# A graph attention kernel: a chunk's last product finished behind the next chunk's first block, its maxima transposed a half-step later, masks and sums loaded earlier

## The chip, the cores and the metric

The kernel runs on one core of a Trainium2 chip. A core has a matrix engine (TensorE, PE in the profile; PEld is its weight load), a vector engine (VectorE, DVE), a scalar engine (ScalarE, ACT), a general engine (GpSimd, POOL) and a queue engine (SyncE, SP) that issues most of the DMAs here. The metric is the time of one execution on the device in microseconds; lower is better.

## What is computed

There are 2708 nodes with 512 features each, and an adjacency matrix `adj` with 0 and 1, about 16 neighbours a node. Four layers follow each other, each with a residual and a layer norm. Layers 0, 1 and 3 multiply by `adj` (scaled by degrees in the first two) and by one 512 x 512 weight. Layer 2 is two attention layers, and this is where the change lies:

```python
def _gat_layer(x, W, adj):
    proj = x @ W
    Wh, Ws = jnp.split(proj, 2, axis=-1)
    scores = Wh @ Ws.T
    a = jax.nn.softmax(scores, axis=-1) * adj
    out = a @ Wh
    out = out + x
    return jax.nn.leaky_relu(out, NEG_SLOPE)
```

The softmax runs over all 2708 nodes before the mask is applied, so all scores must be made, with their maxima and sums; of the products `a @ Wh` only those at neighbours are needed.

## The kernel before, in words

**Tiling.** The nodes are 22 blocks of 128 rows (the last has 20). Their columns are cut into six chunks: 0 to 3 of 512, chunk 4 of 384, chunk 5 of 276. The scores are held transposed: for one chunk of columns, `ch.s[j]` is block j of rows. For each attention layer, `layer` (line 2105) goes through the six chunks, and while the scores of one chunk are made, the chunk before it is finished ("old" in the code), and the gathers of older ones are multiplied.

**The scores.** Chunks 0 to 4 ("seven") use a scheme of seven half products instead of eight. `pair_steps` (line 1694) takes two row blocks at a time, s and r. For a pair t, product numbers stand in `PRODUCTS` (line 1670). Each product is two matrix multiplications over half of the columns. They add up in two PSUM banks: y takes 2 and 3 in one half and 2 and 5 with it (`ahead`, then `six`), and x takes 1, then 6, 7 and 4 in turn. Between two of them ScalarE copies x out, since each partial sum is needed: after 1 and 6 into s, after 7 into v, after 4 into r. VectorE then adds y to s (`first_block`) and v to r (`second_block`). A pair is walked in two half-steps. In the first, `ahead` makes products 2 and 5 of this pair, VectorE runs `first_block` of the pair before, `one` makes product 1, and `four` makes product 4 of the pair two before. In the second, `seven` makes product 7 of the pair before, `six` makes 3 and 6 of this one, and VectorE runs `second_block` of the pair before. Each half-step yields "mid" once and "end" once. There are ten pairs; block 18 ("ALONE") and the small block 21 stand outside. They are made in `scores` (line 1788), ALONE ahead of the pairs and 21 after the first half-step. `walk` (line 2087) puts this in order. After the last pair, products 4 of the pair before, 7 and 4 of the last pair follow directly, and then the next chunk begins.

PSUM has eight banks in two halves of four. y lies in the first half, x in the first half for two pairs in three, and transposes and gathered sums in the second. A new tile takes the bank that has been free longest, and its writer waits for the last reader.

**The half-steps as a clock.** `layer` counts "end" in n: 0 after block ALONE, 1 to 20 for the half-steps, 21 after the last products. At n, besides the scores, it issues for the old chunk:

- `load_mask` (line 1869): four row blocks of the mask, one SP DMA of 256 KB at 512 columns, six a chunk
- `greatest` (line 1818): VectorE's running maximum over the row blocks, `top`. Blocks that are complete wait one call before they are taken, unless `last` is set
- `shift_rows` (line 1839): TensorE transposes `top` (tr_top), VectorE reduces it (mx) and spreads it (wide). `shift_columns` (line 1860): TensorE transposes it back (tr_mx), ScalarE copies it to `shift`
- `soften` (line 1876): one of SOFT = 26 calls. Call v subtracts `shift` from block v (VectorE); ScalarE takes the exponential of block v - 2; VectorE adds block v - 4 to the running sum and multiplies it by its mask, and SP writes it to the table `pairs` in DRAM. At chunk 5, which isn't "seven", nothing changes in this: the distance is that of the old chunk
- `weigh` (line 1989): GpSimd gathers rows of `pairs` by lists of neighbours (`fetch`, g in the profile, at most ten ahead), TensorE multiplies them (acc), VectorE ends the rows (xr, r). The two tables `pairs` are used in turn, so chunk k's writes must wait until chunk k - 2 has been gathered. A planner's clock, advanced by the cost of what TensorE is given, says when a gather counts as landed

For the following chunk it issues `load_moving` (xs, its moving columns, four SP DMAs), `sum_moving` (t1, t2, t4, six VectorE subtractions) and, in `pair_steps`, `load_sums` (s1, s2, s4, sums of weights of a group, three SP DMAs of 256 KB).

**Order.** Every engine and every queue runs its instructions in the order in which the program issues them: `Ordered` (line 54) ties each to the one before it on its engine. So an instruction that waits holds back what was issued after it on the same engine; SP's order holds masks, sums, xs and the writes of `pairs`.

**The end of attention.** After chunk 5 the rest of its softmax, gathers and products runs while TensorE is given other work (`fill`): in the first layer the projections of the second, in the second layer the beginning of layer 3, whose features are split into high and low halves (`halve` (line 749): xh by ScalarE, xl by VectorE) and whose adjacency bytes are cast to m by ScalarE.

In the profile nearly all instructions carry line 71, that of a helper, so its groups are told by the names of tiles.

Of the kernel before, what the change touches and what calls it, by code (L numbers as in the profile page):

```python
# [22 lines left out]
NB = 22  # L23
NP = NB * P
DC = D // P
# [463 lines left out]
SOFT = NB + 2 * 2  # L489
# [919 lines left out]
class Attention:  # L1409
# [7 lines left out]
    def __init__(self, fast):  # L1417
        self.f, self.k, self.nc = fast, fast.k, fast.nc
        self.page, self.bank = fast.page, fast.bank
        tc = self.k.tc  # L1420
        self.scratch = self.k.ctx.enter_context(
            tc.tile_pool(name="pairs", bufs=1, space=DRAM)
        )

        self.pairs = [
            [
                self.scratch.tile([NP, 2 * PAIR + D], FP, tag=f"p{a}{b}", name=f"pairs{a}{b}")
                for b in range(2)  # L1430
            ]
            for a in range(2)
        ]
        self.mixed = self.scratch.tile([DC, P, D], FP, tag="mixed", name="mixed")
        self.quarter = [
            [
                self.scratch.tile(
                    [2, P, pairs_of(k)[0] * P], FP, tag=f"q{a}_{k}", name=f"quarter{a}_{k}"
                )
                for k in range(len(CH))  # L1440
            ]
            for a in range(2)
        ]
        self.sums = [
            [
                self.scratch.tile([3, P, 2, 2 * P], FP, tag=f"u{a}_{k}", name=f"sums{a}_{k}")
                for k in range(STREAMED)
            ]
            for a in range(2)
        ]  # L1450
        self.layers = [AttentionLayer(a, self.pairs[a]) for a in range(2)]
        self.clock, self.fetch_free, self.pending = 0.0, 0.0, []


    def blank(self):
# [238 lines left out]
    def pair_steps(self, ch):  # L1694
# [7 lines left out]
        following = ch.k + 1 in SEVEN  # L1702
# [42 lines left out]
        for n, p in enumerate(pairs):  # L1745
            self.replace(ch.ly, p[0])
            if ch.k == 0 and p[0] in groups and p[1] == 0:
                self.keep_sums(ch.ly, p[0])
            t = begin(n, p)
            ahead(t)  # L1750
            if old:
                first_block(old)
            yield "mid"
            one(t)
            if older:
                four(older)
            if ch.k and p[1] == 0 and p[0] + 1 in groups:
                self.load_sums(ch.ly, p[0] + 1)
            if following and p == pairs[-1]:
                self.load_sums(ch.ly, 0)  # L1760
            yield "end"
            if old:
                seven(old)
            yield "mid"
            six(t)
            if old:
                second_block(old)
            older, old = old, t
            yield "end"
        four(older)  # L1770
        seven(old)
        first_block(old)
        yield "mid"
        four(old)
        second_block(old)
        yield "end"

    def load_moving(self, ch):
# [97 lines left out]
    def soften(self, ch):  # L1876


        nc, v, cw = self.nc, ch.softened, ch.cw
        ch.softened += 1  # L1880
        if v < NB:
            if v == 0 and ch.k >= 2:

                assert not self.chunks[ch.k - 2].to_fetch
            n = rows_of(v)
            s = ch.s[v][:n, :cw]
            nc.vector.tensor_sub(s, s, ch.shift[:n, :cw])
        j = v - ch.apart
        if 0 <= j < NB:
            s = ch.s[j][: rows_of(j), :cw]  # L1890
            nc.scalar.activation(s, s, AF.Exp)
        j -= ch.apart
        if j < 0:
            return
        if j == NB - 1:
            ch.softened = SOFT
        if j % DC == 0 and j + DC < NB:
            self.load_mask(ch, j // DC + 1)
        n = rows_of(j)
        s = ch.s[j][:n, :cw]  # L1900
        if j == 0:
            ch.sum = self.page(f"sum{ch.name}")
            nc.vector.tensor_copy(ch.sum[:, :cw], s)
        else:
            nc.vector.tensor_add(ch.sum[:n, :cw], ch.sum[:n, :cw], s)
        nc.vector.tensor_mul(s, s, ch.masks.pop(j)[:n, :cw])
        to = ch.ly.pairs[ch.k % 2][j * P : j * P + n, :]
        if cw == BANK:
            nc.sync.dma_start(
                to[:, : 2 * PAIR].rearrange("j (r x) -> j r x", x=PAIR)[:, :, D:],  # L1910
                ch.s[j][:n, :].rearrange("j (r x) -> j r x", x=2 * P),
            )
            return
        for r in range(2):
            w = min(2 * P, cw - r * 2 * P)
            nc.sync.dma_start(
                to[:, r * PAIR + D : r * PAIR + D + w],
                ch.s[j][:n, r * 2 * P : r * 2 * P + w],
            )
# [151 lines left out]
    def run(self, next_layer):  # L2071
# [11 lines left out]
        for ly in self.layers:  # L2083
            fill = self.second(chunks[1][0]) if ly.number == 0 else next_layer
            self.layer(ly, chunks[ly.number], fill)

    def walk(self, ch):

        if not ch.seven:
            for j in [0, 1, 2, NB - 1, *range(3, NB - 1)]:  # L2090
                self.scores(ch, j)
                yield "end"
            return
        if not ch.part:
            self.sum_moving(ch)
        self.scores(ch, ALONE)
        yield "end"
        n = 0
        for what in self.pair_steps(ch):
            yield what  # L2100
            n += what == "end"
            if what == "end" and n == 1:
                self.scores(ch, NB - 1)

    def layer(self, ly, chunks, fill):
        f = self.f
        self.chunks, self.made = chunks, {}
        for k, ch in enumerate(chunks):
# [3 lines left out]
            n = -1  # L2112
            for what in self.walk(ch):
                if what == "mid":
                    if old and n >= 2 and old.softened < SOFT:
                        self.soften(old)
                    continue
                n += 1
                if old and n == 0:
                    self.load_mask(old, 0)  # L2120
                    self.greatest(old, last=True)
                if old and n == 3 and k >= 3:
                    while chunks[k - 3].to_weigh:
                        self.weigh(True)
                if old and n >= 3:
                    for _ in range(n % 3 == 0 if ch.seven else 1 + n % 2):
                        if old.softened < SOFT:
                            self.soften(old)
                f.beat()
                if n == 14 and k:  # L2130
                    f.packed(k - 1)
                if following and n == 17:
                    self.load_moving(following)
                if following and following.seven and n == 20:
                    self.sum_moving(following)
                if not following and n in ((5, 11, 19) if ly.number == 0 else (5, 11)):
                    next(fill)
# [7 lines left out]
                for _ in range(3):  # L2145
                    if not self.weigh():
                        break
                if old and n == 1:
                    self.shift_rows(old)
                if old and n == 2:  # L2150
                    self.shift_columns(old)
            assert not old or old.softened == SOFT
        last = chunks[-1]
        self.load_mask(last, 0)
        self.greatest(last, last=True)
        self.until(self.clock + 3, fill)
        self.shift_rows(last)
# [119 lines left out]
```

## Time and profile before

| | |
|---|---|
| median of 3 runs | 2378.08 us (2374.12 to 2386.72) |
| the profiled execution | 2319.82 us |
| its span (first to last instruction) | 2317.6 us |
| attention's scores, layer by layer | about 769 to 1240 us and 1454 to 1933 us |
| mean granted TensorE clock | 0.986 |
| DMA | 523.27 MB, mean 226 GB/s |

The page shows one profiled execution. "Busy" is the share of the span in which an engine had an instruction under way; the ends of matmuls are modelled. In lists of waits, "PE spx <- ACT v" reads: TensorE's matmul that writes spx waited for ScalarE's instruction that wrote v. In a timeline, a line is start, duration, engine, line, operation, output <- inputs, shapes and a count, and in square brackets the idle time of the engine ahead of it with what ended that. Names: sp is a score block made directly; spy and spx are y and x of a pair; tr_top and tr_mx are the transposes of the maxima; a is a mask; g a gather; s<-s,shift, sum<-sum,s and s<-s,a are the three VectorE parts of `soften`; s<-s,spy is `first_block`, s<-s,v is `second_block`.

The chunks of the two layers begin (block ALONE, or the first block of chunk 5) near these times: 769, 837, 906, 1008, 1102 and 1171 us in the first, 1454, 1522, 1591, 1697, 1796 and 1868 us in the second. The profile took a window apart by engine; the prediction uses it.

### The profile page before, as it was taken

How to read it: one execution, taken by the hardware profiler on the slowest of the kernel's cores; microseconds unless marked ns; L12 is line 12 of the kernel's file. 1: busy time of each engine (PE TensorE's matmuls, PEld its weight loads, DVE VectorE, ACT ScalarE, POOL GpSimd, SP SyncE). 2: the span in 40 equal slices, each digit the busy share in tenths (PEclk: the TensorE clock that was granted, in tenths of full speed). 3: DMA queues.
4: the chain of work that ended last, by engine and by line, in shares of the span. 5: the costliest groups of instructions: out<-in, count | busy, mean ns of one | idle time of the engine just before them, and what ended most of it. 6: DMA issues, size and time to landing. Idle time of an engine off the chain costs nothing.

```text
span 2317.6 us, 29497 instructions
## 1 busy us (share of the span) xinstructions
PE 2234.1 (96%) x9724; PEld 1509.8 (65%) x9724; DVE 1549.7 (67%) x3180; ACT 727.9 (31%) x1654; POOL 702.0 (30%) x827
## 2 busy tenths in 40 slices
PE   9999999999999998999999999998999997999997
PEld 6677777777644786676855444786665763476685
DVE  6666787786664769888974522579888985355523
ACT  7444452222111233333422201243333432251211
POOL 2333441111000001635556550001635464643000
PEclk9999999999999999999999999999999998999999
DMA  9965762222557615879999999426978899884311
GB/s 338 280 201 164 191 187 84 76 80 92 208 195 275 213 41 189 313 277 341 318 341 340 364 364 391 167 75 211 309 258 309 314 322 340 260 259 143 112 47 43
DMA packets 285139, 523.27 MB, mean 226 GB/s; under 512 B 42926, under 2 KB 134758, under 8 KB 284976
## 3 DMA queue, kind: packets, MB, share of 16 engines
q1 hardware_dynamic: 216320, 306.34, 38.4%
q0 software_dynamic: 68656, 214.96, 27.9%
q8 instruction: 78, 1.28, 0.2%
q14 instruction: 85, 0.70, 0.1%
HBM read 335.34 MB, written 185.83 MB: 225 GB/s over the span
## 4 chain that ended last, share of the span: by engine, by line
PE 65%; DVE 15%; DMA 13%; issue 3%; ACT 2%; SPq 1%; POOL 1%; DVEq 0%; ACTq 0%; POOLq 0%
PE acc L71 27%; PE spx L71 9%; PE mm L71 8%; PE spy L71 7%; DVE s L71 6%; PE wst L71 5%; PE z L71 5%; DMA g<-pairs,givers 4%; PE sp L71 3%; DVE sum L71 2%; DMA pairs<-s 2%; DVE top L71 1%; DMA pairs<-z_sb 1%; DMA mask<-some 1%; DMA at<-in_adj_t 1%
## 5 line engine op out<-in xcount | busy, mean ns | idle before, releaser
L71 POOL DMA_INDIRECT g<-pairs,givers x510 | 520.4, 1020 | 894.3 <-issue 324.2
L71 PE MATMUL acc<-m,xh 128*128 128x512 f32 (+4 forms) x1584 | 568.7, 380 | 12.3 <-ACT m L71 11.3
L71 PE MATMUL acc<-m,xl 128*128 128x512 f32 (+4 forms) x1584 | 551.7, 366 | 10.1 <-DVE xl L71 10.1
L71 PEld LDWEIGHTS acc<-m,xh 128*128 128x128 f32 (+1 forms) x1584 | 289.4, 189 | 75.8 <-issue 21.2
L71 PEld LDWEIGHTS acc<-m,xl 128*128 128x128 f32 (+1 forms) x1584 | 289.7, 189 | 55.2 <-DVE xl L71 11.0
L71 PE MATMUL acc<-g 128*32 128x512 f32 (+1 forms) x1020 | 287.6, 611 | 11.6 <-DMA g<-pairs,givers 10.6
L71 PE MATMUL mm<-w,ht 128*128 128x512 f32 (+1 forms) x528 | 223.2, 593 | 0.0
L71 ACT CAST m<-at 128x512 fp32r<-128x512 uint8 (+5 forms) x396 | 198.7, 566 | 41.7 <-DMA at<-mask 26.8
L71 DVE TENSOR_TENSOR s<-s,a 128x512 f32<-128x512 f32 (+3 forms) x264 | 166.1, 629 | 55.5 <-DMA a<-mask 46.8
L71 PE MATMUL spx<-xs,wst_sb 128*128 128x256 f32 (+1 forms) x800 | 197.8, 372 | 2.6 <-DVE s L71 2.0
L71 PEld LDWEIGHTS acc<-g 128*32 128x32 f32 (+1 forms) x1020 | 78.7, 135 | 153.4 <-issue 91.8
L71 ACT ACTIVATE s<-s 128x512 f32<-128x512 f32 (+3 forms) x264 | 151.6, 581 | 76.3 <-DVE s L71 76.0
L71 PEld LDWEIGHTS spx<-xs,wst_sb 128*128 128x128 f32 x800 | 146.7, 190 | 41.9 <-ACT s L71 11.8
L71 PEld LDWEIGHTS mm<-w,ht 128*128 128x128 f32 (+1 forms) x528 | 95.8, 186 | 116.5 <-issue 112.8
L71 ACT COPY s<-spx 128x256 f32<-128x256 f32 (+1 forms) x300 | 107.7, 360 | 182.9 <-PE spx L71 182.8
L71 DVE TENSOR_TENSOR s<-s,shift 128x512 f32<-128x512 f32 (+3 forms) x264 | 161.4, 621 | 0.2 <-ACT shift L71 0.2
L71 DVE TENSOR_TENSOR sum<-sum,s 128x512 f32<-128x512 f32 (+4 forms) x252 | 156.6, 622 | 3.6 <-ACT s L71 3.6
L71 DVE TENSOR_TENSOR top<-top,s 128x512 f32<-128x512 f32 (+4 forms) x240 | 149.8, 624 | 4.9
L71 PE MATMUL wst<-xt,mixed 128*128 128x512 f32 (+2 forms) x384 | 151.7, 546 | 0.9 <-DMA xt<-t 0.9
L71 PE MATMUL z<-w,xt 128*128 128x512 f32 (+1 forms) x352 | 150.9, 595 | 0.0
L71 PE MATMUL sp<-xs,wst_sb 128*128 128x276 f32 (+5 forms) x512 | 134.3, 477 | 1.8 <-DMA xs<-t 1.8
L71 POOL DMA_DIRECT2D x<-o x44 | 26.0, 597 | 324.6 <-DVE o L71 320.4
(190 smaller groups left out, 2763.9 us busy)
## 6 DMA issues: line engine op xcount, KB each, us to landing
pairs<-z_sb SPq DMA_DIRECT2D x84, 768.0 KB
pairs<-s SPq DMA_DIRECT2D x168, 256.0 KB
s<-sums SPq DMA_DIRECT2D x96, 256.0 KB
at<-in_adj_t SPq DMA_DIRECT2D x84, 256.0 KB
xres<-x POOLq DMA_DIRECT2D x44, 256.0 KB, 4.8
x<-o POOLq DMA_DIRECT2D x43, 256.0 KB, 3.5
pairs<-s SPq DMA_DIRECT2D x84, 128.0 KB
a<-mask SPq DMA_DIRECT2D x40, 256.0 KB
```

Source lines behind the costliest of these rows:

```text
L71: ins = call(*args, **kw)
```

## The change

- The last product 4 and the last `second_block` of a chunk are no longer issued at its end. They are kept in `self.left` and issued by `end_pair` in the next chunk's walk, right after its first block.
- The last maxima are taken at n = 1 instead of 0, `shift_rows` runs at n = 2 instead of 1, `shift_columns` at 3 instead of 2. Softening begins at the second half-step of the second pair ("mid" at n = 3 instead of 2) and has calls at even n from 4 instead of at n divisible by three from 3. When the new chunk is chunk 5 it begins at n = 4 instead of 3, with one or two calls as before.
- Masks: groups 0 and 1 are loaded at n = 0 and 1, and each later group two groups ahead instead of one. At the end of a layer groups 0 and 1 of the last chunk are loaded together.
- The sums of the first group of the next chunk are loaded at the pair before the last instead of at the last. The next chunk's moving columns are loaded at n = 15 instead of 17, their sums made at 18 instead of 20.
- The loop at n = 3 that issued all remaining products of chunk k - 3 is gone. In its place, ahead of the first write of an old chunk's block to `pairs`, products of the chunk two before it are issued until none of that chunk's gathers is left to issue.

```diff
--- before.py
+++ after.py
@@ -1450,6 +1450,7 @@
         ]
         self.layers = [AttentionLayer(a, self.pairs[a]) for a in range(2)]
         self.clock, self.fetch_free, self.pending = 0.0, 0.0, []
+        self.left = None
 
 
     def blank(self):
@@ -1756,7 +1757,7 @@
                 four(older)
             if ch.k and p[1] == 0 and p[0] + 1 in groups:
                 self.load_sums(ch.ly, p[0] + 1)
-            if following and p == pairs[-1]:
+            if following and p == pairs[-2]:
                 self.load_sums(ch.ly, 0)
             yield "end"
             if old:
@@ -1770,9 +1771,12 @@
         four(older)
         seven(old)
         first_block(old)
-        yield "mid"
-        four(old)
-        second_block(old)
+
+        def rest():
+            four(old)
+            second_block(old)
+
+        self.left = rest
         yield "end"
 
     def load_moving(self, ch):
@@ -1879,9 +1883,6 @@
         nc, v, cw = self.nc, ch.softened, ch.cw
         ch.softened += 1
         if v < NB:
-            if v == 0 and ch.k >= 2:
-
-                assert not self.chunks[ch.k - 2].to_fetch
             n = rows_of(v)
             s = ch.s[v][:n, :cw]
             nc.vector.tensor_sub(s, s, ch.shift[:n, :cw])
@@ -1894,8 +1895,11 @@
             return
         if j == NB - 1:
             ch.softened = SOFT
-        if j % DC == 0 and j + DC < NB:
-            self.load_mask(ch, j // DC + 1)
+        if j == 0 and ch.k >= 2:
+            while self.chunks[ch.k - 2].to_fetch:
+                self.weigh(True)
+        if j % DC == 0 and j + 2 * DC < NB:
+            self.load_mask(ch, j // DC + 2)
         n = rows_of(j)
         s = ch.s[j][:n, :cw]
         if j == 0:
@@ -2084,16 +2088,24 @@
             fill = self.second(chunks[1][0]) if ly.number == 0 else next_layer
             self.layer(ly, chunks[ly.number], fill)
 
+    def end_pair(self):
+        if self.left:
+            self.left()
+            self.left = None
+
     def walk(self, ch):
 
         if not ch.seven:
             for j in [0, 1, 2, NB - 1, *range(3, NB - 1)]:
                 self.scores(ch, j)
+                if j == 0:
+                    self.end_pair()
                 yield "end"
             return
         if not ch.part:
             self.sum_moving(ch)
         self.scores(ch, ALONE)
+        self.end_pair()
         yield "end"
         n = 0
         for what in self.pair_steps(ch):
@@ -2112,26 +2124,23 @@
             n = -1
             for what in self.walk(ch):
                 if what == "mid":
-                    if old and n >= 2 and old.softened < SOFT:
+                    if old and n >= 3 and old.softened < SOFT:
                         self.soften(old)
                     continue
                 n += 1
-                if old and n == 0:
-                    self.load_mask(old, 0)
-                    self.greatest(old, last=True)
-                if old and n == 3 and k >= 3:
-                    while chunks[k - 3].to_weigh:
-                        self.weigh(True)
-                if old and n >= 3:
-                    for _ in range(n % 3 == 0 if ch.seven else 1 + n % 2):
+                if old and n < 2:
+                    self.load_mask(old, n)
+                    self.greatest(old, last=n == 1)
+                if old and n >= 4:
+                    for _ in range(n % 2 == 0 if ch.seven else 1 + n % 2):
                         if old.softened < SOFT:
                             self.soften(old)
                 f.beat()
                 if n == 14 and k:
                     f.packed(k - 1)
-                if following and n == 17:
+                if following and n == 15:
                     self.load_moving(following)
-                if following and following.seven and n == 20:
+                if following and following.seven and n == 18:
                     self.sum_moving(following)
                 if not following and n in ((5, 11, 19) if ly.number == 0 else (5, 11)):
                     next(fill)
@@ -2145,13 +2154,14 @@
                 for _ in range(3):
                     if not self.weigh():
                         break
-                if old and n == 1:
+                if old and n == 2:
                     self.shift_rows(old)
-                if old and n == 2:
+                if old and n == 3:
                     self.shift_columns(old)
             assert not old or old.softened == SOFT
         last = chunks[-1]
         self.load_mask(last, 0)
+        self.load_mask(last, 1)
         self.greatest(last, last=True)
         self.until(self.clock + 3, fill)
         self.shift_rows(last)
```

## The prediction

> **What bounds the kernel now.** I read the page first. TensorE is busy 96% of the span, nothing else comes near, and the clock is full but for one slice.
>
> ```profile
> span 2317.6 us, 29497 instructions
> PE 2234.1 (96%) x9724; PEld 1509.8 (65%) x9724; DVE 1549.7 (67%) x3180; ACT 727.9 (31%) x1654; POOL 702.0 (30%) x827
> PE   9999999999999998999999999998999997999997
> PEclk9999999999999999999999999999999998999999
> ```
>
> So only TensorE's idle time (83.5 us in all) and its half-clock stretches can be won. Next I asked for TensorE's waits in 770 to 1960 us, the attention stage, which the change touches alone. Columns: total us, times, longest.
>
> ```profile
> PE tr_top L71 <- DVE top L71: 12.1, 4, 5.2
> PE spx L71 <- ACT v L71: 10.1, 10, 3.5
> PE acc L71 <- DVE xl L71: 9.9, 1, 9.9
> PE acc L71 <- ACT m L71: 6.4, 1, 6.4
> PE acc L71 <- DMA g<-pairs,givers: 6.1, 6, 2.6
> PE spy L71 <- DMA s<-sums: 3.1, 3, 1.7
> PE sp L71 <- DMA xs<-t: 1.8, 3, 0.9
> ```
>
> These sit almost all at the ten changes of chunk and at the end of attention. Then the windows by chunk, here chunks 1, 2 and 4 of the first layer and one stretch inside a change of chunk (columns after the window: us, then busy us and count of PE, PEld, DVE, ACT, POOL, then granted clock and DMA share):
>
> ```profile
> 837.10:906.00 68.90, 66.98 (x305) 55.25 (x304) 62.45 (x105) 32.07 (x75) 0.00 (x0) 1.00 0.32 100
> 906.00:1007.90 101.90, 94.22 (x410) 64.01 (x409) 84.58 (x144) 30.94 (x74) 48.63 (x48) 0.97 0.85 297
> 1101.80:1170.80 69.00, 68.12 (x386) 55.63 (x385) 65.52 (x119) 29.84 (x78) 40.01 (x37) 1.00 0.94 332
> 915.40:922.30 6.90, 3.98 (x15) 1.79 (x16) 4.81 (x10) 0.00 (x0) 2.99 (x3) 0.51 0.79 240
> ```
>
> VectorE is at 91% in chunk 1 and 95% in chunk 4: there it nearly binds too. The last line shows the clock halved around a pause. The timeline at the change from chunk 1 to 2, and at the end of the second layer, shows who is late:
>
> ```profile
> 904.62 0.37 ACT L71 COPY v<-spx 128x256 f32<-128x256 f32 x1 [0.96 <-PE spx L71]
> 905.05 1.13 PE L71 MATMUL spx<-t,wst_sb 128*128 128x256 f32 x4 [0.46 <-ACT v L71]
> ...
> 915.45 0.68 DVE L71 TENSOR_TENSOR s<-s,a 20x512 f32<-20x512 f32 x1
> 916.06 2.20 DVE L71 TENSOR_TENSOR top<-top,s 128x512 f32<-128x512 f32 x3
> 918.32 1.11 PE L71 MATMUL tr_top<-ident,top 128*128 128x128 f32 x4 [5.18 <-DVE top L71]
> ...
> 1927.92 0.32 SPq L71 DMA_DIRECT2D a<-mask  x1
> 1935.48 0.56 DVE L71 TENSOR_TENSOR s<-s,a 128x384 f32<-128x384 f32 x1 [9.75 <-DMA a<-mask]
> 1949.98 0.80 PE L71 MATMUL acc<-m,xl 128*128 128x512 f32 x1 [9.86 <-DVE xl L71]
> ```
>
> Product 4 of a chunk's last pair waits for ScalarE's copy of product 7 (0.46 us). Five instructions of TensorE later the transposes of the maxima wait 5.18 us, because VectorE is still multiplying the last softened block by its mask at 915.45. Late in attention a mask load issued at 1927.92 holds VectorE until 1935.48, and layer 3's low halves (xl) stand behind it.
>
> **What the Trainium skill says.** "TensorE: Matmul & The Clock Gate", Part 1, says the clock falls to half after about one idle window of 3.4 us. The trace agrees: 0.51 over 6.9 us around the 5.18 us pause, and shorter pauses of 3.45, 3.05 and 2.61 us each carry one. "VectorE: DVE Perf Modes", section on the TRN2 errata, gives 691 ns for an fp32 tensor_tensor of 512; the trace has 0.68 to 0.69, but starts lie only 0.60 to 0.72 apart. "PSUM — Partial Sum Buffer", section on engine and sequencer instructions, says ScalarE and VectorE queues are strict FIFO: the trace agrees at 1935 us, where eight xl wait behind one mask product. "DMA: Bandwidth & Descriptors", Anatomy of one DMA, says that a DMA's wait is held by the issuing sequencer. SP's own waits agree: 52.3 us for DVE s between 1800 and 1960, with mask loads queued behind.
>
> **The change, part by part.** A product (four records, 256 columns) starts every 0.864 us at 797 us; seven make a pair, 6.05 us, walked as two half-steps. The first block of the next chunk (sp, eight records) takes 3.44 us (837.10 to 840.54), or about 2.6 us at 384 columns.
>
> *Product 4 behind the next first block.* Nothing is added: the same four matmuls (0.86), ScalarE copy (0.37) and VectorE addition (0.42) move. Between seven and four now lie 3.44 us of work that needs no copy, so the 10 waits on v (10.1 us) are covered: eight of about 0.45, one of 3.45 (needs all 3.44), one of 3.05 (2.6 covers it but for 0.45). About 9.6 us. The two long ones also hold a half clock of 3.4 us each: windows there have clock 0.64 over 4.7 us with TensorE busy, so 1.7 us lost each, 3.3 together. Value 12.5; bounds 3.6 (the small ones alone, if ScalarE stays blocked behind VectorE) and 13.4.
>
> *Maxima a half-step on.* TensorE gets the small last block (about 0.95) and two products (1.73) ahead of tr_top. That covers the waits of 0.47 and 1.28: 1.75 us. The two of 5.18 us are VectorE's backlog, which doesn't shrink: in 849.0 to 916.1 it is busy 64.4 of 67.1 us. Softening starts perhaps 0.6 us later, since the last block's 3.5 us of VectorE work now comes ahead of the transposed maxima. Last mask product then: 916.06 + 0.6 less the last pair's first addition (0.60), second (0.34) and two maxima (1.3), which now come after it: 914.4. That first addition frees a PSUM bank that product 1 of the next chunk needs: 915.1. TensorE is there at about 910.9, so a wait of some 4.2 us stays, under another name (spx waits for DVE s) and with a half clock. After it come 0.86 + 0.95 + 1.73, the transposes 0.5, two products 1.73: the second pair's product 1 starts near 921 where before it started at 925.75, less some 2 us of half clock. Of these 2.5 us, 1.2 are counted under product 4 and sums. I take 2 each, both layers: 4, with the 1.75 makes 5.5; bounds 0 and 12.1 plus two half clocks (half of 3.98 busy, 2.0 each) = 16.
>
> *Sums one pair earlier.* Three SP loads go out 6 us sooner, ahead of pairs<-s. Two waits of 0.69 go: 1.4. The third, 1.67, is the second group's, which isn't moved. Pages: at most 78 of 87 are live, so three more for a pair and one more mask fit: nothing, or up to 3 us if SP waits for a page with pairs<-s behind it.
>
> *Moving columns at 15, sums of them at 18.* Four SP loads. Chunk 5's in layer 0 were issued at 1161.33 and its last part kept TensorE until 1174.64; two half-steps sooner clears the 1.77 us and a half clock (0.61 over 4.4 us, 1.4): 3. Loads and sums keep their distance of three, so VectorE waits no longer for them. The six subtractions (2.6 us) cost VectorE the same earlier.
>
> *No forced weighing at step 3.* It stalls in chunk 5 alone: 2.61 + 1.7 half clock, 1.22. Later by several steps, when the gathers have landed: I take 3.5 of 5.5; lower bound 0. The new wait: pairs<-s of the old chunk's first block waits on SP for the last gather of the chunk two back, with mask loads behind it; gathers end near 1191 us and the block comes near 1195, so nothing, at worst a few us.
>
> *Masks two groups ahead.* Same six loads a chunk. A load goes out four blocks earlier in SP's order, so the one of 1927.92 goes out right behind layer 3's loads, near 1922.6, and the next near 1932 in place of 1937.49. VectorE's last wait ends near 1938 instead of 1942.88, and xl comes some 4.5 us sooner; with half clock 5. Bounds 0 and 16.2 + 2. Elsewhere mask waits fall where TensorE has other work: nothing.
>
> *Softening at a denser rate.* 26 calls remain, but between step 3 and 20 instead of 2 and 21. A block costs VectorE 1.93 us (subtraction at 897.62, the next at 899.55), a pair's own additions and maxima 2.27. With 3 calls for 2.67 a pair it is 8.06 against 7.4, where TensorE needs 6.05. In walks that VectorE binds, TensorE stalls on its banks mid-walk and has no use for VectorE's leisure later. At most two half-steps, 6 us, in each of chunks 1 and 4; for chunk 1 that is in the sum above. For the others I take 4 in all; bounds 0 and 19.
>
> Sum: 12.5 + 5.5 + 1.4 + 3 + 3.5 + 5 - 4 = 26.9 us. The profiled execution takes 2319.82 us (its span and 2.2 around it), so it would take 2292.9. The median shown is 58.3 above it; I take off the same microseconds: 2378.1 - 27 = **2351**.
>
> **The rivals.** *The waits only change names (2370).* ScalarE's v stays behind a late VectorE, the backlog decides chunk 1 in full, the tail stays bound by DMA. Left: eight times 0.45, 1.4 and 3, so 8 us. For it: VectorE at 91 to 95%. Against: 3.44 us of cover is plain work.
> *All the waits go (2320).* 13.4 + 16 + 1.4 + 3.2 + 5.5 + 18 = 58. Against: VectorE had no idle time in chunk 1.
> *VectorE's denser softening binds (slower, 2392).* Place: chunks 1 to 4, at the additions that free PSUM banks. Loss 2 x 6.05 in chunk 1, 2 x 6.6 in chunk 4, with weighing, 2 x 3 in chunks 2 and 3 of layer 1: 31. Maxima, weighing and tail then gain nothing, so against it stand 12.5 + 1.4 + 3: 14 net loss. It decides once TensorE's waits on DVE s exceed some 17 us more than the 4.4 of now. Against: total VectorE work is unchanged, and PSUM lets it lag about a pair.
>
> **Chances.** Forecast 0.55 (own range 2338 to 2363), names only 0.22 (2362 to 2380), all go 0.11 (2315 to 2338), denser binds 0.12 (2380 to 2410). A measurement of this kernel tells 0.5%, about 12 us, from no change. Faster by more: forecast, all go and a fifth of names only, 0.70; slower by more: two thirds of the last, 0.08; the rest 0.22. Range 2328 to 2384: it cuts about half of all-go and most of the last.
>
> **What would show it.** Right: no waits of spx on ACT v at chunk ends; tr_top waits under 1 us, with waits of spx on DVE s near 4 us in their place after chunk 1; no sp wait on xs near 1170; the acc wait on xl near 5 us. Wrong: new waits of spy and spx on DVE s inside walks over 9 us a chunk, SP waiting on gathers with VectorE on masks, or chunks 1 and 4 longer than 68.9 and 69.0 us.

## The result, and the profile after

The kernel after takes 2344.77 us (median; 2340.95 to 2348.78), beside it the kernel before 2379.68 (2374.12 to 2386.72): a ratio of 0.985, 95% interval 0.982 to 0.989. That is 34.9 us less; the forecast was 27 less.

One thing has to be known before any two times are compared: the runs of a group share one chip, and the unchanged kernel before took 2379.7, 2397.7 and 2385.1 us in three groups but 2319.4 and 2318.0 in two, so each kernel is set only against the runs of before in its own group.

The page of before (span 2317.6) is of the second sort, the first page of after (span 2339.0) of the first: subtracted from each other they would say 21 us slower. So the page of after used here is another one, from a group where before takes 2318.0 us (median). There after takes **2292.46** (median), 25.5 us less. The ratio on record for this group is 0.9908 (0.9886 to 0.9930), or 16 to 26 us; the two medians alone divide to 0.9890, which lies inside that interval. The prediction had worked out 2292.9 for such an execution. The page (label e5 below), to be laid beside that of before:

```profile
span 2288.4 us, 29486 instructions
PE 2215.9 (97%) x9724; PEld 1505.2 (66%) x9724; DVE 1547.3 (68%) x3180; ACT 727.7 (32%) x1654; POOL 718.4 (31%) x827
PE   9999999999999998999999999998999997999997
PEclk9999999999999999999999999999999998999999
```

The span is 29.2 us shorter. TensorE's idle time falls by 11.0 us (83.5 to 72.5), its busy time by 18.2 (2234.1 to 2215.9) with the same 9724 matmuls. Of these 18.2, 8.0 are the gathered products (acc<-g, 287.6 to 279.6; the reason is found at e4). Another part is the clock. In this pair of profiles the mean granted clock rises from 0.986 to 0.993, so the full-speed time lost falls from 0.014 x 2317.6 = 32 us to 16. But that is these two executions more than the change: over all runs of the group the mean clock is 0.989 for before and 0.990 for after, an estimate of some 25 and 22 us lost, so the clock makes some 3 us of the difference there.

The Trainium skill, "TensorE: Matmul & The Clock Gate", Part 1, says that the clock falls to half after about one idle window of 3.4 us. The trace agrees for the pause of 3.46 us below (clock 0.72 over the 7 us around it). In before, shorter pauses, of 2.61 and 3.05 us, brought a half clock too (0.62 and 0.64 over the 4.5 and 4.7 us around them), so here 3.4 us are not the least that is needed.

TensorE's waits in the attention stage of after (766 to 1956 us; columns as before: total, times, longest):

```profile
PE spx L71 <- DVE s L71: 9.9, 6, 3.8
PE acc L71 <- DVE xl L71: 9.6, 1, 9.6
PE spy L71 <- DVE s L71: 8.6, 3, 3.5
PE acc L71 <- DMA g<-pairs,givers: 5.6, 10, 1.1
PE acc L71 <- ACT m L71: 5.2, 1, 5.2
PE spy L71 <- DMA s<-sums: 3.1, 3, 1.6
PE spx L71 <- ACT v L71: 2.4, 2, 1.8
```

The waits of tr_top on top (12.1) are gone, and those of spx on v fell from 10.1 us to 2.4. What is left of these stands one product earlier: 1.78 us at 1768.29, ahead of the last product 4 that is still made inside the walk. In their place stand 18.5 us of waits on DVE s, 4.4 before. The one for xl is as long as it was (9.6 and 9.9).

The windows by chunk: chunks 1, 2 and 4 of the first layer, and then 7 us in the middle of chunk 1 (columns as in the prediction):

```profile
831.17:905.00 73.83, 69.18 (x305) 57.18 (x304) 64.15 (x109) 31.99 (x75) 0.00 (x0) 0.95 0.37 113
905.00:999.68 94.68, 92.73 (x410) 63.51 (x409) 81.52 (x138) 31.01 (x74) 52.05 (x48) 1.00 0.85 301
1094.05:1165.50 71.45, 69.75 (x393) 55.77 (x392) 65.32 (x117) 29.99 (x78) 41.98 (x39) 1.00 0.94 333
884.00:891.00 7.00, 3.54 (x11) 2.64 (x10) 6.89 (x13) 1.82 (x5) 0.00 (x0) 0.72 0.31 96
```

Chunk 1 is 4.9 us longer than before, chunk 2 is 7.2 shorter, chunk 4 is 2.5 longer. The timeline of chunk 1 and the start of chunk 2 shows what took the place of the 5.18 us at tr_top:

```profile
880.35 1.13 PE L71 MATMUL spx<-xs,wst_sb 128*128 128x256 f32 x4 [1.19 <-DVE s L71]
888.40 2.07 PE L71 MATMUL spy<-xs,wst_sb 128*128 128x256 f32 x4 [3.46 <-DVE s L71]
912.61 1.13 PE L71 MATMUL spx<-xs,wst_sb 128*128 128x256 f32 x4 [1.42 <-DVE s L71]
```

So VectorE's backlog now stops TensorE in the middle of the walk, at a PSUM bank that VectorE has still to read, with VectorE busy 6.89 of 7 us and the clock at 0.72. Chunks 1 and 2 together are 2.3 us shorter than before (168.5 against 170.8), but it is the same backlog.

By stage, before and then after: scores of layer 0 (from its first block to that of chunk 5), from there to the first block of layer 1, scores of layer 1, and the rest. The columns are those of the windows above; what counts is the length, PE's busy time, and the clock, third from the end.

```profile
767.64:1170.79 403.15, 389.85 (x1867) 295.85 (x1864) 334.20 (x582) 145.06 (x358) 137.26 (x133) 0.99 0.70 244
1170.79:1455.66 284.87, 279.60 (x927) 133.89 (x926) 120.46 (x260) 49.38 (x112) 122.37 (x123) 0.99 0.98 355
1455.66:1867.95 412.29, 392.92 (x1789) 293.66 (x1785) 344.97 (x612) 145.07 (x352) 138.42 (x133) 0.98 0.70 240
1867.95:2317.60 449.65, 412.39 (x1704) 266.20 (x1703) 216.71 (x479) 120.19 (x260) 137.95 (x150) 0.97 0.56 186
```

```profile
763.31:1165.50 402.19, 391.29 (x1870) 296.68 (x1867) 332.96 (x580) 144.99 (x357) 144.32 (x135) 0.99 0.71 247
1165.50:1439.34 273.84, 273.19 (x925) 133.94 (x923) 121.50 (x261) 49.60 (x113) 121.36 (x122) 1.00 0.99 366
1439.34:1844.99 405.65, 385.77 (x1792) 289.96 (x1789) 343.98 (x612) 144.13 (x351) 149.01 (x136) 1.00 0.71 247
1844.99:2288.40 443.41, 409.39 (x1701) 266.87 (x1699) 215.90 (x479) 120.71 (x261) 137.75 (x148) 0.97 0.55 185
```

The gain by stage is 1.0, **11.0**, 6.6 and 6.2 us. (The first score block also comes 4.3 us earlier. Both kernels issue the same instructions up to there, and in the profiles of this study it came anywhere between 760 and 770 us, mostly earlier where the first blocks of the adjacency had landed earlier, at 92 to 99 us. So 4.3 of the 29.2 us are chance.) The largest gain is not where product 4 and the maxima are, but in chunk 5 of layer 0 and after it, where the prediction had only the forced weighing and xs.

### The profile page after: what moved, and what is told of

It is laid out like the page before. It is cut to its first block, busy times and chain, and to the rows that moved or that the text cites. A ratio compares the mean times of both kernels' runs of the same rounds, so it can differ in the third digit from the quotient of the medians.

```text
span 2339.0 us, 29486 instructions
## 1 busy us (share of the span) xinstructions
PE 2237.2 (96%) x9724; PEld 1515.8 (65%) x9724; DVE 1547.5 (66%) x3180; ACT 725.9 (31%) x1654; POOL 717.8 (31%) x827
## 4 chain that ended last, share of the span: by engine, by line
PE 71%; DVE 13%; issue 6%; DMA 6%; ACT 2%; POOL 1%; SPq 1%; another core or an unknown queue 0%; DVEq 0%; ACTq 0%; POOLq 0%
PE acc L71 27%; PE spx L71 10%; PE mm L71 8%; PE spy L71 8%; PE z L71 6%; PE wst L71 6%; DVE s L71 5%; PE sp L71 3%; DVE sum L71 2%; DMA at<-in_adj_t 1%; DVE top L71 1%; DMA g<-pairs,givers 1%; DMA x<-in_x 1%; DMA x<-x 1%; DVE r L71 1%
## 5 line engine op out<-in xcount | busy, mean ns | idle before, releaser
L71 POOL DMA_INDIRECT g<-pairs,givers x510 | 535.8, 1051 | 912.5 <-issue 359.3
L71 PEld LDWEIGHTS acc<-m,xl 128*128 128x128 f32 (+1 forms) x1584 | 288.3, 188 | 54.7 <-DVE xl L71 10.4
L71 PEld LDWEIGHTS spx<-xs,wst_sb 128*128 128x128 f32 x800 | 149.3, 193 | 47.2 <-issue 14.8
L71 DVE TENSOR_TENSOR s<-s,a 128x512 f32<-128x512 f32 (+3 forms) x264 | 166.0, 629 | 18.5 <-issue 9.5
L71 PE MATMUL spy<-xs,wst_sb 128*128 128x256 f32 (+1 forms) x480 | 121.9, 377 | 9.4 <-DVE s L71 9.2
L71 PE MATMUL sp<-xs,wst_sb 128*128 128x276 f32 (+5 forms) x512 | 129.1, 460 | 0.0
```

The costliest lines, as they stand in the source:

```text
L71: ins = call(*args, **kw)
```

## The experiments

The question was which parts make the gain. **Theory A** is the prediction's sum: pauses at the changes of chunk. **Theory B** is that it is made where transfers fill the queues, by when masks and writes go out. **Theory C** was that part of it is chance ahead of attention.

**Both kernels again, side by side.**

> The kernel before, unchanged, once more with a profile, because the profile shown of before (2319.8 us) lies 58 us under its own timed runs, while the profile of after (2341.1 us) is one of its timed runs. If that first profile was an odd execution, this one shows a span near 2375 us, with more or longer TensorE pauses at changes of chunk and in gathers than the 83.5 us of idle time shown, and half-clock stretches beside them. If the two chips or executions simply differ, it shows about 2320 us again, and then the changed kernel beside it decides. Time against before: 1.00.

> The changed kernel, unchanged, on the same chip. My theory: 1.2 to 1.5% faster than before, by the pauses of product 4, of the maxima and of the forced products. Rival: the two profiles shown say the opposite (2339.0 against 2317.6 us of span), so on a chip where before takes 2320 us this takes about 2340 us and is slower by 0.9%.

Measured: before against itself 1.0015 (0.9987 to 1.0042), at 2404.5 us; after 0.9825 (0.9783 to 0.9867), at 2358.0, beside 2397.7. The gain of the first measurement came back. The extra time of this group against before's first page lies mostly in the walks: layer 0's scores took 449.1 us in this profile of before and 431.7 in that of after (403.2 in the first page), layer 1's 437.7 and 422.8 (412.3). What that is, is taken up at the end.

**Each part alone**, in a group where before takes 2319.35 us.

e1: product 4 and `rest` moved behind the next first block, nothing else. The last half-step's softening call goes with the "mid" that it hung on, so one is added:

```diff
-        yield "mid"
-        four(old)
-        second_block(old)
+        def rest():
+            four(old)
+            second_block(old)
+        self.left = rest
...
-                    for _ in range(n % 3 == 0 if ch.seven else 1 + n % 2):
+                    for _ in range(n % 3 == 0 or n == 20 if ch.seven else 1 + n % 2):
```

> The kernel before with product 4 behind the next chunk's first block and nothing else (one more softening call at n = 20, since the last half-step of a chunk that yielded one is gone). Theory A (the prediction's sum: pauses at chunk changes): 12.5 us less than before, 0.5%, and no wait of spx on ACT v at chunk ends. Theory B (the gain comes in chunks 3 to 5, where transfers fill the queues, and comes from when masks, writes and gathers go out): 0 to 5 us less. Theory C (7 to 8 us of the gain lie ahead of the first score block, where both kernels issue the same instructions): the first score block starts near 768 us, as in before, unless the place of the gain is chance, then anywhere between 760 and 768.

Measured: 2319.13 us, 1.0001 (0.9986 to 1.0017). Nothing. TensorE's waits in this profile, 755 to 1960 us:

```profile
PE tr_top L71 <- DVE top L71: 13.3, 7, 3.0
PE spx L71 <- DVE s L71: 6.2, 4, 2.0
PE spx L71 <- ACT v L71: 3.1, 2, 1.8
```

The waits on v fell by 7.0 us (forecast: all 10.1 but 0.45). But tr_top now waits seven times in place of four and spx on s 6.2 us in place of 2.0, with a new 1.7 us on t: added up, 26.6 us with the spy waits on s, before 26.6. TensorE is there sooner, and VectorE is not. (Its first score block came at 765.3 us, so for that place theory C is right: chance.) The longest wait on v shows it already in before:

```profile
1692.45 1.28 ACT L71 ACT_TABLE_LOAD   x1
1695.82 0.21 ACT L71 ACTIVATE rs_t<-rs_v 128x4 f32<-128x4 f32 x1 [2.09 <-DVE rs_v L71]
1695.93 0.35 ACT L71 COPY v<-spx 128x256 f32<-128x256 f32 x1
1696.34 1.28 PE L71 MATMUL spx<-t,wst_sb 128*128 128x256 f32 x4 [3.45 <-ACT v L71]
```

ScalarE's copy takes 0.35 us; it is late because rs_t, a step of the layer norm of finished rows, is ahead of it on ScalarE, with a table load, and waits 2.09 us for VectorE's rs_v. The wait of 3.05 us at 1794.95 has the same cause (1.69 us for rs_v).

e2: the maxima and the softening alone.

```diff
-                    self.greatest(old, last=True)
+                if old and n < 2:
+                    self.greatest(old, last=n == 1)
...
-                    if old and n >= 2 and old.softened < SOFT:
+                    if old and n >= 3 and old.softened < SOFT:
...
-                if old and n >= 3:
-                    for _ in range(n % 3 == 0 if ch.seven else 1 + n % 2):
+                if old and n >= 4:
+                    for _ in range(n % 2 == 0 if ch.seven else 1 + n % 2):
```

(`shift_rows` and `shift_columns` move by one step as in the change.)

> The kernel before with the maxima a half-step on and softening denser (steps 3 to 20 in place of 2 to 21), and nothing else. Theory A: 5.5 gained, 4 lost, so 1 to 2 us less than before; the wait of tr_top on top of over 5 us after chunk 1 gone. Theory B: earlier ends of the old chunk's blocks bring earlier writes, which free pages and let gathers start: 10 to 20 us less, in chunks 3 to 5. The denser softening binding: 10 or more us longer, in waits of spx and spy on DVE s inside the walks.

Measured: 2313.44 us, 0.9960 (0.9946 to 0.9975), 6 to 13 us less. Of its waits on top 2.0 us are left and of v 5.1, the longest 0.5: the two long waits on v are gone although product 4 has not moved, since rs_t now waits only 0.48 and 0.86 us for VectorE. Waits on s make 15.2. Against before, chunk 1 is 4.5 us longer in layer 0 and 5.5 in layer 1, chunk 4 4.4 and 2.8; chunk 2 is 7.5 and 11.2 shorter. That fits a cost of the denser softening in chunks 1 and 4 which the maxima pay back in chunk 2, but the two were not tried apart, and this profile is of e2's longest run (2318.8 us).

e3: masks two groups ahead alone.

```diff
-        if j % DC == 0 and j + DC < NB:
-            self.load_mask(ch, j // DC + 1)
+        if j % DC == 0 and j + 2 * DC < NB:
+            self.load_mask(ch, j // DC + 2)
...
+                if old and n == 1:
+                    self.load_mask(old, 1)
...
         self.load_mask(last, 0)
+        self.load_mask(last, 1)
```

> The kernel before with masks loaded two groups ahead, two together at a layer's end, and nothing else. Theory A: 5 us less, all of it at the wait of acc on xl after the last chunk of the second layer, nothing in the walks. Theory B: masks are late where transfers fill the queues, so 10 to 20 us less, in the walks of chunks 3 to 5.

Measured: 2310.35 us, 0.9954 (0.9936 to 0.9971), 7 to 15 us less. VectorE's waits for masks in 755 to 2075 us, in before and then here:

```profile
DVE s L71 <- DMA a<-mask: 46.8, 11, 13.2
```

```profile
DVE s L71 <- DMA a<-mask: 11.6, 3, 5.8
```

The stages say where: 5.8 us of it between chunk 5 and layer 1, 2.6 in the rest, 0.4 and 0.9 in the scores. Neither theory had the place right. xl still waits 10.4 us, so A's wait didn't shrink either. In chunk 5 of layer 0 TensorE's waits for xs (1.8 us in before) and for a gather of the forced weighing (2.6) are 0 and 0.2 us in this profile, and its clock from the first block to tr_top is 1.00 in place of 0.95. How an earlier mask shortens them is not shown.

e4: the forced weighing taken out, the `while` ahead of the first write put in.

```diff
-                if old and n == 3 and k >= 3:
-                    while chunks[k - 3].to_weigh:
-                        self.weigh(True)
...
+        if j == 0 and ch.k >= 2:
+            while self.chunks[ch.k - 2].to_fetch:
+                self.weigh(True)
```

> The kernel before without the forced weighing at n = 3 of a walk (gathers still to be issued are issued ahead of the first write to their table) and nothing else. Theory A: 3.5 us less, at chunk 5 of either layer. Theory B: in the executions that take 2390 us or more the gathers are later than in the one first profiled, so forced weighing stalls longer: 10 us or more less, in chunks 3 to 5.

Measured: 2318.97 us, 0.9997 (0.9982 to 1.0011). Nothing; xl and den, the sums of the softmax, wait longer in this profile (15.5 and 4.2 us), which is of one of the longer runs (2327.5).

One saving shows all the same, and not in TensorE's idle time. In the removed loop the gathered products wait for their gathers pair by pair, while the profile counts TensorE as busy. Two rows of e3, which has the loop, and one of e5, which hasn't:

```profile
1179.28 6.40 PE L71 MATMUL acc<-g 128*32 128x512 f32 x12 [0.23 <-DMA g<-pairs,givers]
1180.39 0.14 PEld L71 LDWEIGHTS acc<-g 128*32 128x32 f32 x2 [0.97 <-DMA g<-pairs,givers]
```

```profile
1180.43 1.06 PE L71 MATMUL acc<-g 128*32 128x512 f32 x8
```

From the first block of chunk 5 of layer 0 to its tr_top, 48 such products count 10.6 us in before and 11.6 in e3, but 6.4 in e4, e5 and e8. So e4 saves some 4 to 5 us of TensorE there, but its profile has longer waits on den and xl after it, and its time is no shorter.

By their ratios the parts measured alone make 0, 9, 11 and 1 us, 21 together, and the ratio of the whole is worth 21 too (16 to 26); by the medians they make 0, 6, 9 and 0, 15 together, against 25.5. So whether the parts are worth more together than one by one can't be told from these sums. Sums and moving columns were not tried alone.

**Each part taken out of the changed kernel**, in another group (before 2318.01 us). Each kernel is the change without the lines of e1, e2 or e3; without the maxima, a softening call at n = 20 makes up for the "mid" that product 4 took with it.

> The changed kernel itself, beside three kernels that each take one of its parts out. So far the parts alone, where before takes 2319 us: product 4 0, maxima 6 less, masks 9 less, no forced weighing 0. If the parts add up: 15 us less than before, ratio 0.9935 (0.65%). If product 4 pays only together with the maxima (alone its waits moved on to tr_top): 25 us or more less, ratio 0.989 or below. If before takes near 2390 us here, as where the ratio was 0.9825: 35 to 42 us less.

> The changed kernel with product 4 and its addition back at the end of a chunk, all else as changed. Parts that add up: as the changed kernel, within 3 us. Product 4 paying only together with the maxima: 7 to 12 us longer than the changed kernel, and ten waits of spx on ACT v of 5 to 10 us together.

> The changed kernel with the maxima at n = 0, 1, 2 and softening at the old rate again (one call more at n = 20, since the last half-step that yielded one is gone). Parts that add up: 6 us longer than the changed kernel. Together with product 4: 12 to 18 us longer, the waits of tr_top on DVE top back at 12 us or more.

> The changed kernel with masks one group ahead again. Parts that add up: 9 us longer than the changed kernel. The prediction's sum: 5 us longer, all at the end of the second layer. If the denser softening already does what the earlier masks do: within 3 us.

| | median us | ratio to before | interval |
|---|---|---|---|
| e5, the changed kernel | 2292.46 | 0.9908 | 0.9886 to 0.9930 |
| e6, without product 4 | 2299.31 | 0.9927 | 0.9904 to 0.9949 |
| e7, without the maxima | 2297.63 | 0.9922 | 0.9902 to 0.9942 |
| e8, without the masks | 2315.09 | 0.9995 | 0.9978 to 1.0012 |

Only e8 stands apart from e5: the masks are worth 22.6 us by the medians (the means lie 21.6 apart, with an interval of some 17 to 26), more than the 7 to 15 that they made alone, and without them nothing that can be measured is left of the rest. Product 4 and the maxima are worth 6.9 and 5.2 by the medians, with intervals that overlap that of e5, so their size is not settled. Their waits came back as expected: 7.4 us of spx on v in e6, 16.6 of tr_top on top in e7. The profiles put product 4's part in the walks (e6 against e5: 4.8 and 3.9 us longer in the two layers' scores), where it had made nothing alone; that it needs the maxima out of its way fits e1, but the runs only suggest it.

Why the masks are worth more here than alone shows in chunk 5 of layer 0, from its first block to its own tr_top, where all work of the layer's scores ends:

| | first block to tr_top, us |
|---|---|
| before | 74.0 |
| e3, masks alone | 69.6 |
| e8, all but the masks | 73.0 |
| e5, all | 65.4 |

In before, TensorE lost time there to xs, to the forced weighing and their half clock, and came to tr_top without a wait. Without these losses it comes sooner, and finds VectorE behind a mask. (e5 is 4.2 us shorter than e3 because its gathered products take less, as at e4; neither waits at tr_top.) The timeline of e8, SP's mask loads and what waits (lines of other instructions left out):

```profile
1210.71 0.64 SPq L71 DMA_DIRECT2D a<-mask  x1
...
1220.34 0.56 DVE L71 TENSOR_TENSOR s<-s,a 128x384 f32<-128x384 f32 x1 [6.49 <-DMA a<-mask]
1221.42 0.49 SPq L71 DMA_DIRECT2D a<-mask  x1
...
1228.88 0.56 DVE L71 TENSOR_TENSOR s<-s,a 128x384 f32<-128x384 f32 x1 [1.75 <-DMA a<-mask]
...
1237.92 0.98 DVE L71 TENSOR_TENSOR top<-top,s 128x276 f32<-128x276 f32 x2
...
1239.05 0.87 PE L71 MATMUL tr_top<-ident,top 128*128 128x128 f32 x3 [6.74 <-DVE top L71]
```

A mask load takes 9.6 and 7.5 us here from its issue to the product that waits for it, with DMA busy 0.95 of this stage. One group ahead is a lead of four products, and these follow each other at 1.5 to 1.9 us, so some 7 us in the program: too short. It is less on the chip, because SP has an order too. The first load belongs to the product at 1206.64 and leaves at 1210.71, behind eight other transfers (w and t) on SP, when VectorE is 3.1 us from needing it. Two groups ahead is a lead twice as long. After e8's tr_top come 3.35 us of den, and at the end of layer 1 the same chain once more:

```profile
1912.39 0.32 SPq L71 DMA_DIRECT2D a<-mask  x1
...
1924.00 0.56 DVE L71 TENSOR_TENSOR s<-s,a 128x384 f32<-128x384 f32 x1 [13.40 <-DMA a<-mask]
1925.12 0.52 ACT L71 ACTIVATE s<-s 128x384 f32<-128x384 f32 x1 [14.16 <-DVE s L71]
...
1936.15 0.80 PE L71 MATMUL acc<-m,xh 128*128 128x512 f32 x1 [14.62 <-ACT m L71]
```

The mask holds VectorE 13.4 us, VectorE holds ScalarE's exponential, the casts to m stand behind that on ScalarE, and TensorE waits 14.62 us for m. Here the order of SP weighs most: the load belongs to the product at 1903.37, leaves SP 9.0 us later behind other transfers (at and x), and VectorE has been waiting for it since 1910.60. In e5 the same three waits are 5.70, 6.99 and 5.19 us, and that load too left SP late, 8.4 us after its product.

By stage e8 is longer than e5 by 0.3, 15.3, 0.4 and 8.4 us: nearly all of it at the two ends of layers, nothing in the walks. Against before it is shorter by 0.6 us in the walk of layer 0 and 6.2 in that of layer 1, and longer by 4.3 and 2.2 at the two ends: what the other parts win in the walks is lost again behind the masks.

**Two parts, and a longer lead.** This group fell where before takes 2385.09 us. e9 has e2 and e3 together. e10 is the changed kernel with masks three groups ahead:

```diff
+                if old and n < 3:
+                    self.load_mask(old, n)
                 if old and n < 2:
-                    self.load_mask(old, n)
                     self.greatest(old, last=n == 1)
...
-        if j % DC == 0 and j + 2 * DC < NB:
-            self.load_mask(ch, j // DC + 2)
+        if j % DC == 0 and j + 3 * DC < NB:
+            self.load_mask(ch, j // DC + 3)
...
         self.load_mask(last, 1)
+        self.load_mask(last, 2)
```

> The kernel before with two of the parts: masks two groups ahead, and the maxima a half-step on with denser softening. Where before takes 2319 us: if these two add up as they did alone, 15 us less (ratio 0.9935). If earlier masks are what lets every other part pay, so that each part taken out of the changed kernel is worth what its absence cost there (product 4 costs 7 and the maxima 5 by their absence, so some 14 of 25.5 us come from the masks and the parts not taken out): 14 to 19 us less, and the waits of spx on ACT v at chunk ends stay at 5 to 10 us. If these two are all there is: 25 us less, as the changed kernel. Where before takes near 2390 us, the same order with larger sizes (the changed kernel there: 0.9825).

> The changed kernel with masks three groups ahead (groups 0, 1 and 2 at n = 0, 1 and 2, three together at a layer's end), one page more. In the changed kernel VectorE still waits 5.7 us for a mask near the end of the second layer, and TensorE 5.2 us for m behind it. If the lead of the masks still decides: 5 to 8 us less than the changed kernel, ratio to before near 0.988 where before takes 2319 us. If two groups are enough and the end is bound by what VectorE has to do: no difference. If the pages run out: longer, with waits of ACT s for writes to pairs.

Measured: e9 2339.35 us, 0.9830 (0.9787 to 0.9874); e10 2346.63 us, 0.9826 (0.9795 to 0.9857). Both are where the changed kernel was in such groups, 0.9825 and 0.985. So masks and maxima are enough for the whole gain as far as these intervals of some 7 to 10 us to each side tell, and a third group of lead brings nothing that can be measured. Neither was tried where before takes 2318 us.

## Why the prediction was right, and where it was not

The sign, the time (2351 against 2344.8) and the sum (26.9 against 25.5 by the medians, or 21 by the ratio, where before takes 2318) were right. But the sum is right by luck: its largest term made nothing alone, and the terms for the masks and the maxima were too small by about as much.

- **Product 4 behind the next first block, 12.5: failed.** (Its own terms, 9.6 and 3.3, add up to 12.9.) Its waits on v went for the most part, and alone it is worth 0 (0.9986 to 1.0017), in the changed kernel 6.9 by the medians, not settled. The step that failed is the cover: 3.44 us of TensorE work hide ScalarE's copy, but whoever is late next is VectorE, and TensorE only reached it sooner. And 9.4 of the 12.5 us (3.45, 2.6 and the half clocks of 3.3) hung on two waits that were VectorE's from the start, as rs_t shows, and that e2 is rid of without moving product 4. The prediction named this rival ("the waits only change names") and set it at 0.22 for the whole; for this part, alone, it is what happened.
- **Maxima a half-step on, 5.5, less 4 for the denser softening: too small.** Alone 9.3 by the ratio (5.8 to 12.5), 5.9 by the medians. (The 5.5 counts 2 us for each layer, where its own working, 2.5 less 1.2, leaves 1.3.) The place was right: tr_top's waits went, and a wait of spx on DVE s came after chunk 1, forecast at 4.2 us and found at 1.4 in layer 0 and 3.8 in layer 1. Chunks 1 and 4 got longer than 68.9 and 69.0, named as a sign against the forecast: over both layers they lost 11.7 us in e5. Chunk 2 gave back 13.9, which that sign left out.
- **Masks two groups ahead, 5: the main error.** 10.7 alone by the ratio (6.7 to 14.8), 22.6 by the medians in the changed kernel. "Elsewhere mask waits fall where TensorE has other work: nothing" failed. It was untrue already in before, where e3 won 5.8 us between chunk 5 and layer 1, and more so once the same change made TensorE earlier, where e8 loses 15.3 us there. The trace of before had the sign: 46.8 us of VectorE's waits for masks, 28.5 of them at 1231 to 1332 us. The term was priced by TensorE's waits alone, and edits that share an end were priced one by one.
- **xl: near 5 forecast, 9.6 found.** xl itself came sooner by 6.2 us, counted from chunk 5's first block (82.0 to 75.9), forecast 4.5. But TensorE came sooner by as much, so the wait kept its length. A shorter wait was the wrong thing to look for; the stage is 6.2 us shorter.
- **No forced weighing, 3.5:** alone 0.7 (-2.5 to 4.2). Its wait is gone from the changed kernel. The term counted idle time and half clock only, and left out the 4 to 5 us in which TensorE counts as busy. **Sums and moving columns, 4.4:** the wait on xs is gone, but e3 lost it without moving them; on sums 3.1 us stay, as many as before, so the 1.4 us forecast there did not come. Their sizes alone were not measured.
- **Pages and the loads of SP:** "nothing" stands. ScalarE waits for pages that a write to `pairs` still holds 4.5 us in e5, 4.4 before. (The 1.78 us at 1768.29 are not of these: there rs_t waits 2.15 us for VectorE.)
- **Denser softening binds (2392):** it was to decide from some 17 us more of TensorE's waits on DVE s. There are 14.1 more, close to that line, and yet the time fell.

## What to carry to other kernels

A removed wait is worth what the next late engine leaves of it: list, for each, who is late next, and by how much, before it is counted. Edits that end at the same meeting point are priced together, since one that looks like nothing (a load earlier for an engine that is not the bottleneck) can decide what all the others are worth. A lead of loads is counted in time, not in groups: from when the queue really issues the load, which its order can put 4 to 9 us late as here, to when its reader needs it. And a busy share can hide a wait, where instructions follow each other only as fast as their inputs come.

## What the runs showed of the hardware

The same program took 2318 to 2319 us in two groups of runs and 2380 to 2398 in three, 2.6 to 3.5% apart, with the runs of before in each group within 1.2% of each other. Each chip on record was used by one group only, so whether this goes with the chip or with the time of the run is open. Transfers were hardly slower: the packets took 1545 us of each DMA engine in the first page of before and 1560 in the slower one. Of the 85.5 us more of span, 71.4 lie in the scores of the two layers. In layer 0 TensorE is idle 28.9 us more and busy 17.1 us more, at a clock of 0.95 in place of 0.99. Some of it is pauses in which TensorE, VectorE and ScalarE stand still together while gathers go on. One in the profile of before at 2405 us, first as a window, then as a timeline:

```profile
1139.00:1146.00 7.00, 0.01 (x1) 0.00 (x0) 0.00 (x0) 0.85 (x2) 5.18 (x6) 0.66 1.02 377
```

```profile
1145.73 0.32 ACT L71 COPY s<-spx 128x192 f32<-128x192 f32 x1 [5.82 <-issue]
1146.08 0.56 DVE L71 TENSOR_TENSOR s<-s,spy 128x384 f32<-128x384 f32 x1 [9.43 <-issue]
1146.11 1.65 PE L71 MATMUL spx<-xs,wst_sb 128*128 128x192 f32 x4 [7.09 <-issue]
```

"issue" says that no releaser is on record; ScalarE's copy waits for a product that was over at 1139.0. In such profiles some two fifths of the semaphore events are missing (4,254 recorded in the scores of layer 0 against 6,998 in the first page), so whether the signals themselves are late or only their records are lost stays open, and nothing here was built on who released whom in them. In these groups the gain of the change lies in the walks too (17.4 and 14.9 us of the two layers' scores, between the profiles of before at 2405 us and of after at 2359 in the same group); which of the parts makes it there was not tried one by one.
